# Moving a head's turned squares: sixteen transfers between partitions in place of a trip through DRAM

## The chip, the cores and the metric

The kernel runs on one core of one Trainium2 chip. The metric is the device time of one execution in microseconds. A core has five instruction queues that run beside each other and meet at semaphores: PE (matrix products, with its weight loads shown as PEld), DVE (elementwise and reductions), ACT (activation functions), POOL (GpSimd) and SP, which here only issues DMA transfers. The transfers run on sixteen DMA engines that all queues share.

## The reference, cut to what matters

Two transformer layers on 8 sequences of 512 tokens of 256 elements, in float32. Layer 0 is a rotary scan attention followed by a mixture of 16 experts with a shared expert. Layer 1 is causal attention with 16 heads of 128, followed by a feed-forward whose weights are looked up in a table of 16 values:

```python
# layer 1, attention (x: 8 x 512 x 256)
k = jnp.einsum('ihd,bpd->biph', W_K, x)
q = jnp.einsum('ihd,bpd->biph', W_Q, x)
v = jnp.einsum('ihd,bpd->biph', W_V, x)
scores = jnp.einsum('biph,biqh->biqp', k, q)
masked = scores * mask - 1e10 * (1.0 - mask)
attn = softmax(masked / sqrt(d_head), axis=-1)
z = jnp.einsum('biqp,biph->biqh', attn, v)
out = jnp.einsum('df,bqf->bqd', W_O, z_flat)
# layer 1, feed-forward
w = lut[idx]          # for gate, up and down: 688x256, 688x256, 256x688
```

The change lies in the attention of layer 1: 8 sequences x 16 heads = 128 heads.

## The kernel before, in words

Layer 0 comes first. From about 580 to 2010 us of the profiled execution the attention of layer 1 runs, in a software pipeline that is written out by hand: within it, PE, DVE, POOL and SP each keep the order of the program, and only ACT's order is left to a scheduler. The last part, some 230 us, is the feed-forward.

The outer loop goes over 64 pairs of heads (`p`), the inner one over the two heads of a pair (`e`). What a head goes through is spread over three turns of this loop; `front` is the head of the turn before, `rear` the one before that.

- `scores(i)`, for four row tiles i of 128 queries: PE makes the scores `sc` of the causal part (128 x 128(i+1)), DVE adds the mask, scales and takes the minimum of the negated row into `low`, writing `ms`; ACT exponentiates `ms` into `pr[i]` and sums the rows into `den`. `ms` has two buffers, each `pr[i]` one.
- `normalized(...)`: DVE takes reciprocals, and ACT scales the rows of `pr` into `slots`, a buffer (two of them) of 128 partitions x 4 x 10 x 32: ten squares of 128 x 128 for the causal half, cut into pieces of 32 columns.
- `squares_turned()`, for `front`, one turn later: DVE transposes each 32 x 32 block of `slots` in place (L1127). What is then still to be done is an exchange of whole blocks between groups of 32 partitions. SP writes `slots` to the DRAM tile `squares` in four transfers of 160 KB (L1130).
- `exchanged()`, later in the same turn: SP waits for those four to land and reads `squares` back into `pT` in one transfer of 640 KB (L1135). `pT` has one buffer.
- `weigh()`, for `rear`, another turn later: PE multiplies `v` with `pT` into `pz` (L1159), and ACT copies the result into `zT`.

Only the last two heads go another way, by PE transposes (`turned`), so 126 heads use the squares. Each turn also holds a share of the projections of the following pair (`pairs`, `groups`, L239), and of the output projection of the quarter of heads that was finished before (`one_out`, L1213).

SP issues the weights in the same order of the program (`load_weights`, L739 to L745; `w` for queries and keys, `wv`, `wo`), at the calls of `load_following`. `wo` has one buffer: it is loaded when the last product of a quarter (`products(3)`, within `one_out`) has been issued, and the next turn's `one_out` (`products(0)`) needs it. In such a turn the program's order is: `scores(0)` and `scores(1)`, `squares_turned`, `one_out` with the load of `wo`, ..., `scores(2)` and `scores(3)`, `exchanged`, the other loads. The framework gives the DMAs of SP eight completion semaphores in turn; a DMA that takes one again waits until the one that had it before has landed.

POOL forms the sums that the output projection takes (`zS`, L1190 to L1193), gathers rows, and once per turn takes a step of `lookups`, which builds the tables `fs` and `fd` of the feed-forward from indices: for each of 16 values a comparison (`tmp`, L956) and an addition (L959). For `fs` an operation spans 688 columns, and one value is a step; for `fd` 256 columns, and two values are a step.

Of the kernel before, what the change touches and what calls it, by code (L numbers as in the profile page):

```python
# [10 lines left out]
F32 = mybir.dt.float32  # L11
I32 = mybir.dt.int32
AF = mybir.ActivationFunctionType
# [4 lines left out]
P = 128  # L18
NB, T, D = 8, 512, 256
# [10 lines left out]
INTER = 688  # L30
# [10 lines left out]
SQ = 32  # L41
NQ = P // SQ

SLOT = {(j, i): n for n, (j, i) in enumerate((j, i) for j in range(NT) for i in range(j, NT))}
NS = len(SLOT)
# [70 lines left out]
def two_layers(ctx: ExitStack, tc: tile.TileContext, a: dict, out: bass.AP):  # L116
    nc = tc.nc
# [112 lines left out]
    class Sevens:  # L230


        def __init__(self, operands, out):
            self.operands, self.out = operands, out
# [102 lines left out]
    for b in range(1, NB):  # L337
# [8 lines left out]
            out=xs[NE * REG : NE * REG + NE * P, :].rearrange("(n p) d -> p n d", p=P),  # L346
            in_=zero.unsqueeze(1).to_broadcast([P, NE, D]),
# [377 lines left out]
    sv = tc.dram_tile([NGRP, P, 5 * 2 * DH], F32, name="sv")  # L725
    so = tc.dram_tile([NGRP, P, 5 * 2 * DH], F32, name="so")


    squares = [tc.dram_tile([P, NQ, NS * SQ], F32, name=f"squares{n}") for n in range(2)]

    wtp = ctx.enter_context(tc.tile_pool(name="wt", bufs=1))

    plain = {n: a["aqk"][n] for n in range(2)} | {"v": a["av"], "o": a["ao"]}
# [2 lines left out]
    def load_weights(n, part, first):  # L736
        f = 2 * DH if n in ("v", "o") else DH
        w = wtp.tile([P, 7, f], F32, tag=f"w{n}", name=f"w{n}", bufs=1 if n in ("v", "o") else 2)
        nc.sync.dma_start(out=w[:, :2, :], in_=plain[n][part, :, : 2 * f].rearrange("p (k f) -> p k f", k=2))  # L739
        rest = w[:, 2:, :]  # L740
        kept = made[n][part].rearrange("p (k f) -> p k f", k=5)
        if not first:
            nc.sync.dma_start(out=rest, in_=kept)
            return w, None
        nc.sync.dma_start(out=w[:, 5:, :], in_=plain[n][part, :, 2 * f :].rearrange("p (k f) -> p k f", k=2))  # L745

        return w, (lambda *eng: sums(w, *eng), lambda eng=nc.sync: eng.dma_start(out=kept, in_=rest))
# [66 lines left out]
    with tc.tile_pool(name="lk", bufs=2, side="right") as lkp, tc.tile_pool(  # L814
        name="xb", bufs=4, side="right"
# [49 lines left out]
        xb, xbT, h, hT = {}, {}, {}, {}  # L865
        weights = {}
        with tc.manual_schedule(engines={ENG.PE}):
            for s in range(NBLK + 5):
                if s % VB == 0 and s < NBLK:
                    n = min(VB, NBLK - s)  # L870
# [12 lines left out]
                if s % 12 == 2 and 0 < s // 12 <= 5:  # L883
                    n, part = ((0, 0), (1, 0), ("v", 0), (0, 1), (1, 1))[s // 12 - 1]
                    w, complete = load_weights(n, part, True)
# [40 lines left out]
    fs = w2.tile([P, 7, INTER], F32, name="fs")  # L926
# [6 lines left out]
    def lookups(pool):  # L933

        parts = [
            (fs[:, n, :], a[f"idx{w}"][c * P : (c + 1) * P, :], P)
            for n, w, c in ((W_1, 0, 0), (W_2, 0, 1), (W_4, 1, 1), (W_3, 1, 0))
        ]
        behind = []
        parts += [(fd[:k, i, :], a["idx2"][r : r + k, :], k) for i, (r, k) in enumerate(ICH)]  # L940

        def indices(dst, src, k):
            idx = pool.tile([P, INTER], I32, tag="idx", name="idx")
            nc.gpsimd.dma_start(out=idx[:k, : src.shape[1]], in_=src)
            return idx

        idx = indices(*parts[0])
        yield
        for m, (dst, src, k) in enumerate(parts):
            n = src.shape[1]  # L950
            for v in range(NLUT):
                if v == 0:
                    nc.gpsimd.tensor_scalar(dst, idx[:k, :n], 0.0, lut[:k, 0:1], ALU.is_equal, ALU.mult)
                else:
                    tmp = pool.tile([P, INTER], F32, tag="tmp", name="tmp")
                    nc.gpsimd.tensor_scalar(  # L956
                        tmp[:k, :n], idx[:k, :n], float(v), lut[:k, v : v + 1], ALU.is_equal, ALU.mult
                    )
                    nc.gpsimd.tensor_add(dst, dst, tmp[:k, :n])  # L959
                if v == NLUT - 1 and m + 1 < len(parts):  # L960
                    following = indices(*parts[m + 1])
                if n > T or v % 2:
                    if behind:
                        behind.pop(0)()
                    yield
            if dst is parts[3][0]:
                for n, c, at in ((W_1, 0, APART), (W_2, 1, APART), (W_4, 1, 0), (W_3, 0, 0)):
                    nc.gpsimd.tensor_copy(over[:, c, at : at + OVER], fs[:, n, NF * P :])
                behind = sum_steps(fs[:, :, : NF * P], nc.gpsimd)
            idx = following  # L970
# [3 lines left out]
    with tc.tile_pool(name="big", bufs=2, side="right") as big, tc.tile_pool(  # L974
        name="a1", bufs=1, side="right"
    ) as ap1, tc.tile_pool(name="lk", bufs=1, side="right") as lkp, tc.tile_pool(
        name="a2", bufs=2, side="right"
    ) as ap2, tc.tile_pool(name="pj", bufs=1, space=PSUM) as pj, tc.tile_pool(
        name="psc", bufs=2, space=PSUM
    ) as psc, tc.tile_pool(name="ptt", bufs=2, space=PSUM) as ptp, tc.tile_pool(  # L980
        name="pz", bufs=1, space=PSUM
    ) as pzp, tc.tile_pool(name="po1", bufs=1, space=PSUM) as pop:
        look = lookups(lkp)

        class Sequence:
# [87 lines left out]
                return self.v[:, j % 2, 2 * (e // 2) + j // 2, (e % 2) * DH : (e % 2 + 1) * DH]  # L1073

        class Head:
            def __init__(self, qT, kT, v, z, place, by_slots):
                self.by_slots = by_slots
                self.qT, self.kT, self.v, self.z = qT, kT, v, z
                self.pr, self.squares = {}, squares[place]
                self.low = small.tile([P, NT], F32, name="low", bufs=3)  # L1080
                self.den = small.tile([P, NT], F32, name="den", bufs=3)
                self.rd = small.tile([P, NT], F32, name="rd", bufs=3)

            def scores(self, i):

                kw = (i + 1) * P
                sc = psc.tile([P, T], F32, tag="sc", name="sc")
                nc.tensor.matmul(sc[:, :kw], self.qT[:, i * P : kw], self.kT[:, :kw], start=True, stop=True)  # L1088
                ms = ap2.tile([P, T], F32, tag="ms", name="ms")
                low = self.low[:, i : i + 1]  # L1090

                nc.vector.tensor_tensor_reduce(  # L1092
                    out=ms[:, :kw],
                    in0=sc[:, :kw],
                    in1=mask[:, T - kw :],
                    scale=-1.0 / math.sqrt(DH),
                    scalar=3e38,
                    op0=ALU.add,
                    op1=ALU.min,
                    accum_out=low,  # L1100
                )
                pr = self.pr[i] = ap2.tile([P, kw], F32, tag=f"pr{i}", name="pr", bufs=1)
                nc.scalar.activation(pr, ms[:, :kw], AF.Exp, bias=low, scale=-1.0, accum_out=self.den[:, i : i + 1])  # L1103

            def normalized(self, *tiles):

# [17 lines left out]

            def squares_turned(self):

                nc.vector.transpose(self.slots, self.slots)  # L1127
                to, slots = self.squares.rearrange("(n k) q s -> q k n s", n=NQ), self.slots.rearrange("p n s k -> p n (s k)")
                for q in range(NQ):
                    nc.sync.dma_start(out=to[q], in_=slots[q * SQ : (q + 1) * SQ])  # L1130

            def exchanged(self):

                self.pT = ap1.tile([P, NQ, NS, SQ], F32, name="pT")
                nc.sync.dma_start(out=self.pT.rearrange("p q s k -> p q (s k)"), in_=self.squares)  # L1135

            def turned(self):

                nc.vector.reciprocal(self.rd, self.den)
                self.pT = ap1.tile([P, NQ, NS, SQ], F32, name="pT")  # L1140
                for i in range(NT):
                    nc.scalar.activation(self.pr[i], self.pr[i], AF.Copy, scale=self.rd[:, i : i + 1])
                for j in range(NT):
                    pt = ptp.tile([P, T], F32, tag="pt", name="pt")
                    for i in range(j, NT):
                        nc.tensor.transpose(pt[:, i * P : (i + 1) * P], self.pr[i][:, j * P : (j + 1) * P], ident)
                    (nc.scalar.copy if j % 2 else nc.vector.tensor_copy)(
                        self.of_keys(j), pt[:, j * P :].rearrange("p (i q k) -> p i q k", q=NQ, k=SQ)
                    )
# [134 lines left out]
        for c in (1, 2, 4, 6):  # L1284
# [14 lines left out]
            out=mask[:, T - P :],  # L1299
            in_=mask[:, T - P :],  # L1300
# [6 lines left out]
        with tc.manual_schedule(engines={ENG.PE, ENG.DVE, ENG.Pool, ENG.SP}):  # L1307
# [18 lines left out]
            front = rear = None  # L1326
            for p in range(ALL):
# [4 lines left out]
                if pair % 2 == 0:  # L1332
                    z = big.tile([P, VG, T], F32, tag="big", name="zT")
                for e in range(2):
# [1 line left out]
                        *(pairs[p].of_head(n, e) for n in range(2)),  # L1336
                        lambda j, g=groups[p // 2], h=2 * (p % 2) + e: g.of_head(j, h),
                        z[:, 2 * (pair % 2) + e, :],
                        e,
                        p < ALL - 1,  # L1340
                    )
                    in_time()
# [31 lines left out]
                        one_out()  # L1374
                    head.scores(2)
                    head.scores(3)
                    if front and front.by_slots:
                        front.exchanged()
                    load_following()
                    in_time()  # L1380
                    if e and ahead:
# [12 lines left out]
                    front, rear = head, front  # L1394
# [29 lines left out]
    with tc.tile_pool(name="f1", bufs=1) as f1, tc.tile_pool(  # L1424
        name="f2", bufs=2
    ) as f2, tc.tile_pool(name="f3", bufs=3) as f3, tc.tile_pool(name="ft", bufs=1, space=PSUM) as ft, tc.tile_pool(
        name="fp", bufs=3, space=PSUM
# [65 lines left out]
        with tc.manual_schedule(engines={ENG.PE}):  # L1493
            for b in range(NB + 1):
                q = seqs[b] if b < NB else None
                front = seqs[b - 1] if b else None
# [127 lines left out]
```

## Time and profile before

| | us |
|---|---|
| median of 2 runs | 2252.16 (2249.09 to 2255.24) |
| the profiled execution | 2247.57 |
| its span, first to last instruction | 2245.8 |
| PE busy | 2108.6 (94%) |
| DVE busy | 1539.8 (69%) |
| ACT busy | 1184.2 (53%) |
| POOL busy | 868.7 (39%) |
| pT and squares of a head: first and last issue | 581.4 and 1988.0 |
| mean granted clock of PE | 0.993 of full speed |

DMA moved 363.99 MB, 162 GB/s in the mean; of HBM 241.29 MB were read and 120.72 MB written.

How to read it: busy time says how long an engine's instructions lasted, not what the time depends on. A line of waits names the engine and instruction that waited, what ended the wait, the sum in us, the number of times and the longest. `L1159` is line 1159 of the kernel before; `pT<-squares` is a transfer that writes pT and reads squares; SPq is a DMA issue on SP, whose duration is the time that it held the queue, not that of the transfer.

### The profile page before, as it was taken

The page shows a single profiled execution, that of the slowest core. Times are in us where ns is not written, and L with a number is a line of the kernel's source. Part 1 is how long each engine was busy: PE and PEld are TensorE (multiplying, and loading weights), DVE is VectorE, ACT ScalarE, POOL GpSimd, SP SyncE. Part 2 cuts the span into 40 slices and gives each one's busy share as a digit, 9 for nine tenths or more (in the row PEclk, how much of TensorE's full clock was granted, in tenths as well). Part 3 has the DMA queues.
Part 4 walks back from the last instruction along what each step waited for, and adds up shares of the span by engine and source line. Part 5 has one row for each costly group of instructions (what it writes and reads, how often), then busy time and mean ns, then how long its engine had stood idle before and what let it go on. Part 6 is the DMA issues. An engine that isn't in the chain of part 4 may idle for free.

```text
span 2245.8 us, 29655 instructions
## 1 busy us (share of the span) xinstructions
PE 2108.6 (94%) x8733; PEld 1546.5 (69%) x8733; DVE 1539.8 (69%) x3950; ACT 1184.2 (53%) x2943; POOL 868.7 (39%) x767
## 2 busy tenths in 40 slices
PE   6999998999799999999999999999999999989999
PEld 3554545886576767777777767777677777758887
DVE  6788887555567767666767766766766766758765
ACT  5767762333465556555556555556555555643211
POOL 0022233001464474565466456654535445330000
PEclk9999999999999999999999999999999999999999
DMA  6111216552567666766666666675756665520000
GB/s 194 46 69 64 75 68 238 182 162 90 168 223 229 217 208 206 221 196 218 202 213 200 221 207 207 199 227 175 216 185 208 201 219 181 177 93 11 19 19 29
DMA packets 207873, 363.99 MB, mean 162 GB/s; under 512 B 27120, under 2 KB 145264, under 8 KB 207712
## 3 DMA queue, kind: packets, MB, share of 16 engines
q1 hardware_dynamic: 197712, 333.62, 47.0%
q0 software_dynamic: 8704, 27.42, 3.6%
q8 instruction: 70, 1.15, 0.2%
q10 hardware_dynamic: 1296, 1.06, 0.1%
q14 instruction: 91, 0.75, 0.1%
HBM read 241.29 MB, written 120.72 MB: 161 GB/s over the span
## 4 chain that ended last, share of the span: by engine, by line
PE 67%; DMA 15%; DVE 12%; ACT 3%; issue 3%; SPq 1%; POOL 0%; DVEq 0%; POOLq 0%; ACTq 0%
PE pb L239 14%; PE pz L1159 11%; PE pa L239 10%; PE sc L1088 9%; DMA pT<-squares 9%; PE po L1213 6%; PE py L1482 4%; PE pgu L841 3%; DMA scale<-dscale 2%; PE pyb L859 2%; DMA squares<-slots 1%; DVE slots L1127 1%; DVE v L379 1%; PE pa L432 1%; DMA wo<-in_ao 1%
## 5 line engine op out<-in xcount | busy, mean ns | idle before, releaser
L1123 ACT ACTIVATE slots<-pr,rd 128x128 f32<-128x128 f32 x756 | 302.3, 463 | 187.1 <-DVE rd L1111 112.4
L1159 PE MATMUL pz<-pT,v 128*128 128x512 f32 (+3 forms) x1024 | 308.0, 445 | 44.9 <-DMA pT<-squares 44.8
L1088 PE MATMUL sc<-qk,qk 128*128 128x128 f32 (+3 forms) x1024 | 318.4, 433 | 0.9 <-DVE low L1092 0.8
L1159 PEld LDWEIGHTS pz<-pT,v 128*128 128x128 f32 x1024 | 194.3, 193 | 170.5 <-issue 65.6
L1103 ACT ACTIVATE pr<-ms,low 128x128 f32<-128x128 f32 (+3 forms) x512 | 282.3, 552 | 51.6 <-DVE low L1092 49.5
L1092 DVE CUSTOM_DVE_ANT_0 ms<-sc,mask 128x128 f32<-128x128 f32 (+3 forms) x512 | 238.0, 483 | 63.0 <-PE sc L1088 56.8
L956 POOL TENSOR_SCALAR tmp<-idx,lut 128x256 f32<-128x256 int32 (+2 forms) x150 | 259.5, 1730 | 12.5
L1127 DVE STREAM_TRANSPOSE slots<-slots 128x1280 f32<-128x1280 f32 x126 | 190.2, 1510 | 103.3 <-ACT slots L1123 102.3
L1166 ACT COPY zT<-pz 128x512 f32<-128x512 f32 x128 | 74.9, 585 | 288.5 <-PE pz L1159 284.5
L239 PE MATMUL pb<-tT,w 128*128 128x256 f32 x762 | 207.4, 381 | 6.3 <-DVE qk L253 5.0
L1088 PEld LDWEIGHTS sc<-qk,qk 128*128 128x128 f32 x1024 | 172.5, 191 | 47.6 <-ACT slots L1123 1.6
L632 POOL DMA_INDIRECT xs<-xn,slot x64 | 79.7, 1246 | 311.2 <-DVE share L642 121.6
L262 DVE TENSOR_TENSOR qk<-pb,u 128x512 f32<-128x512 f32 x127 | 85.3, 672 | 140.6 <-PE pb L239 140.6
L1190 POOL TENSOR_TENSOR zS<-zT 128x512 f32<-128x512 f32 x31 | 40.7, 1314 | 329.1 <-PE po L1213 329.0
L251 DVE TENSOR_TENSOR u<-pa,p 128x256 f32<-128x256 f32 x230 | 96.9, 421 | 89.7 <-ACT p L249 83.2
L239 PEld LDWEIGHTS pb<-tT,w 128*128 128x128 f32 x762 | 139.4, 191 | 25.5 <-DVE qk L253 7.5
L239 PE MATMUL pa<-xT,w 128*128 128x256 f32 x508 | 151.1, 379 | 0.0
L893 POOL DMA_INDIRECT yg<-ys,yrow x64 | 65.0, 1016 | 187.8 <-PE pu L190 138.9
L1213 PE MATMUL po<-zS,wo 128*128 128x256 f32 x512 | 125.9, 379 | 1.2 <-DVE kept L1224 1.2
L252 DVE TENSOR_TENSOR p<-pb,u 128x256 f32<-128x256 f32 x230 | 97.6, 424 | 25.2 <-DVE u L251 1.8
L1213 PE MATMUL po<-zT,wo 128*128 128x256 f32 x384 | 97.0, 390 | 17.3 <-DMA wo<-in_ao 17.3
L239 PE MATMUL pb<-wv,tT 128*128 128x256 f32 x378 | 103.8, 383 | 8.3 <-DVE qk L262 8.1
(315 smaller groups left out, 4306.3 us busy)
## 6 DMA issues: line engine op xcount, KB each, us to landing
squares<-slots SPq DMA_DIRECT2D x504, 160.0 KB
pT<-squares SPq DMA_DIRECT2D x126, 640.0 KB
w<-sqk SPq DMA_DIRECT2D x112, 320.0 KB
w<-in_aqk SPq DMA_DIRECT2D x144, 128.0 KB
wv<-sv SPq DMA_DIRECT2D x28, 640.0 KB
wo<-so SPq DMA_DIRECT2D x28, 640.0 KB
xb<-xs SPq DMA_DIRECT2D x79, 128.0 KB
ys<-yb SPq DMA_DIRECT2D x79, 128.0 KB
```

Of the source, the lines that this page charges most:

```text
L239: nc.tensor.matmul(to, lhsT, rhs, start=first, stop=True, skip_group_check=True)
L251: nc.vector.tensor_tensor(self.u2, pa[:, 1, :], p1, ALU.add)
L252: nc.vector.tensor_tensor(p1, pb[:, 0, :], self.u2, ALU.add)
L956: nc.gpsimd.tensor_scalar(tmp[:k, :n], idx[:k, :n], float(v), lut[:k, v : v + 1], ALU.is_equal, ALU.mult)
L1088: nc.tensor.matmul(sc[:, :kw], self.qT[:, i * P : kw], self.kT[:, :kw], start=True, stop=True)
L1092: nc.vector.tensor_tensor_reduce(out=ms[:, :kw], in0=sc[:, :kw], in1=mask[:, T - kw :], scale=-1.0 / math.sqrt(DH), scalar=3e38, op0=ALU.a ...
L1103: nc.scalar.activation(pr, ms[:, :kw], AF.Exp, bias=low, scale=-1.0, accum_out=self.den[:, i : i + 1])
L1123: nc.scalar.activation(to, pr, AF.Copy, scale=rd)
L1127: nc.vector.transpose(self.slots, self.slots)
L1159: nc.tensor.matmul(pz[:, :, j:, :].rearrange("p q i k -> p q (i k)"), self.v(j), self.pT[:, :, SLOT[j, j] : SLOT[j, j] + NT - j, :].rearra ...
L1213: nc.tensor.matmul(po[:, m, :], self.w[:, n, k * P : (k + 1) * P], self.sides[n][:, k, :], start=(k == 0), stop=(k == 1),)
L1482: nc.tensor.matmul(py, self.h[:, i, t * P : (t + 1) * P], fd[:, i, :], start=(i == 0), stop=(i == NI - 1))
```

## The change

The DRAM tile `squares` and the call of `exchanged` go. After the DVE transpose SP issues sixteen transfers, each from the 32 partitions of one group of `slots` to the 32 partitions of one group of `pT` (1280 bytes per partition, 40 KB in all). `pT` moves from the pool with one buffer to that with two. `ms` goes: the masked scores are written to `pr`, and the exponential works in place. The lookups of `fs` are cut into halves of 344 columns, so that `idx` and `tmp` take half the memory; two values are then a step everywhere. The lines behind these move up by 3 to 6.

```diff
-    squares = [tc.dram_tile([P, NQ, NS * SQ], F32, name=f"squares{n}") for n in range(2)]
...
         parts = [
-            (fs[:, n, :], a[f"idx{w}"][c * P : (c + 1) * P, :], P)
+            (fs[:, n, h : h + INTER // 2], a[f"idx{w}"][c * P : (c + 1) * P, h : h + INTER // 2], P)
             for n, w, c in ((W_1, 0, 0), (W_2, 0, 1), (W_4, 1, 1), (W_3, 1, 0))
+            for h in (0, INTER // 2)
         ]
...
-            idx = pool.tile([P, INTER], I32, tag="idx", name="idx")
+            idx = pool.tile([P, INTER // 2], I32, tag="idx", name="idx")
...
-                    tmp = pool.tile([P, INTER], F32, tag="tmp", name="tmp")
+                    tmp = pool.tile([P, INTER // 2], F32, tag="tmp", name="tmp")
...
-                if n > T or v % 2:
+                if v % 2:
...
-            if dst is parts[3][0]:
+            if dst is parts[7][0]:
...
-            def __init__(self, qT, kT, v, z, place, by_slots):
+            def __init__(self, qT, kT, v, z, by_slots):
...
-                self.pr, self.squares = {}, squares[place]
+                self.pr = {}
...
-                ms = ap2.tile([P, T], F32, tag="ms", name="ms")
+
+                pr = self.pr[i] = ap2.tile([P, kw], F32, tag=f"pr{i}", name="pr", bufs=1)
                 low = self.low[:, i : i + 1]
 
                 nc.vector.tensor_tensor_reduce(
-                    out=ms[:, :kw],
+                    out=pr,
...
-                pr = self.pr[i] = ap2.tile([P, kw], F32, tag=f"pr{i}", name="pr", bufs=1)
-                nc.scalar.activation(pr, ms[:, :kw], AF.Exp, bias=low, scale=-1.0, accum_out=self.den[:, i : i + 1])
+                nc.scalar.activation(pr, pr, AF.Exp, bias=low, scale=-1.0, accum_out=self.den[:, i : i + 1])
...
             def squares_turned(self):
 
+
                 nc.vector.transpose(self.slots, self.slots)
-                to, slots = self.squares.rearrange("(n k) q s -> q k n s", n=NQ), self.slots.rearrange("p n s k -> p n (s k)")
+                self.pT = ap2.tile([P, NQ, NS, SQ], F32, name="pT")
                 for q in range(NQ):
-                    nc.sync.dma_start(out=to[q], in_=slots[q * SQ : (q + 1) * SQ])
-
-            def exchanged(self):
-
-                self.pT = ap1.tile([P, NQ, NS, SQ], F32, name="pT")
-                nc.sync.dma_start(out=self.pT.rearrange("p q s k -> p q (s k)"), in_=self.squares)
+                    for n in range(NQ):
+                        nc.sync.dma_start(
+                            out=self.pT[n * SQ : (n + 1) * SQ, q], in_=self.slots[q * SQ : (q + 1) * SQ, n]
+                        )
 
             def turned(self):
 
                 nc.vector.reciprocal(self.rd, self.den)
-                self.pT = ap1.tile([P, NQ, NS, SQ], F32, name="pT")
+                self.pT = ap2.tile([P, NQ, NS, SQ], F32, name="pT")
...
-                    if front and front.by_slots:
-                        front.exchanged()
                     load_following()
```

More of the change, by code (lines that the diff above doesn't have):

```diff
@@ L1338, in two_layers @@
                         z[:, 2 * (pair % 2) + e, :],
-                        e,
                         p < ALL - 1,
```

## The prediction

> **What bounds the kernel now.** I read the page from its top. PE is busy for 94% of the span, and the chain that ended last runs over PE for two thirds and over DMA for 15%, most of it pT:
>
> ```profile
> PE 2108.6 (94%) x8733; PEld 1546.5 (69%) x8733; DVE 1539.8 (69%) x3950; ACT 1184.2 (53%) x2943; POOL 868.7 (39%) x767
> ...
> PE 67%; DMA 15%; DVE 12%; ACT 3%; issue 3%; SPq 1%; POOL 0%; DVEq 0%; POOLq 0%; ACTq 0%
> ```
>
> The chain's DMA share is no saving: when a transfer goes from the chain, the chain follows PE's work instead. What can be saved is what PE waits, so the waits of PE and of its weight loads come next:
>
> ```profile
> PEld pz L1159 <- DMA pT<-squares: 57.9, 39, 5.3
> ...
> PE pz L1159 <- DMA pT<-squares: 44.8, 34, 4.9
> ...
> PEld po L1213 <- DMA wo<-in_ao: 21.8, 20, 1.8
> ...
> PE po L1213 <- DMA wo<-in_ao: 17.3, 20, 3.4
> ```
>
> PE loses some 45 us to pT, which the change shortens, and 17 us to wo, which is loaded through the same SP queue. So the question is not only when pT lands, but what SP does first. One head in the timeline (start, duration, engine; the bracket is idle time and what ended it):
>
> ```profile
> 1210.27 1.51 DVE L1127 STREAM_TRANSPOSE slots<-slots 128x1280 f32<-128x1280 f32 x1
> ...
> 1211.84 1.87 SPq L1130 DMA_DIRECT2D squares<-slots  x4
> ...
> 1213.76 0.70 SPq L739 DMA_DIRECT2D wo<-in_ao  x1
> ...
> 1214.51 0.66 SPq L743 DMA_DIRECT2D wo<-so  x1
> ...
> 1216.27 0.32 SPq L1135 DMA_DIRECT2D pT<-squares  x1
> ...
> 1217.88 1.99 PE L1213 MATMUL po<-zT,wo 128*128 128x256 f32 x8 [0.89 <-DMA wo<-in_ao]
> ...
> 1222.29 2.42 PE L1159 MATMUL pz<-pT,v 128*128 128x512 f32 x8 [0.69 <-DMA pT<-squares]
> ```
>
> Call the first squares issue t0 (1211.84). Four squares issues take 1.88 us, 0.47 each; the last has landed at about t0+4.3, where SP goes on to pT; pT lands just before t0+10.45. wo is issued at t0+1.92, **behind the squares in SP's order**, lands just before t0+6.04, and PE stands waiting for it. I went through the timeline head by head in this way (126 heads, 11.2 us apart in the mean). In 23 of the handovers of wo from one quarter to the next it is like this one: issue near t0+1.95, PE's first product near t0+6.15, nearly always after a wait; pz follows 3.7 us after that product began. Seven others are loaded 29 us or more before their use. The pz waits split into 13.5 us in those 23 heads and 31.2 us in the other 103.
>
> **The change part by part.**
>
> *Transfers.* Out go 126 x 4 squares issues, 126 pT issues, SP's wait between them, and the second trip of 655 KB per head. In come 126 x 16 issues of 41 KB (32 partitions x 1280 B), partition to partition. DMA bytes fall by 126 x 0.655 = 83 MB of 364; that saves PE nothing by itself, as the DMA engines are busy only some 0.65 in this stage.
>
> What one of the sixteen costs SP is not in the trace. The near rows are:
>
> ```profile
> L1130 SPq DMA_DIRECT2D squares<-slots x504: 302/433/1737, 581.4 to 1982.9; - x168
> L1135 SPq DMA_DIRECT2D pT<-squares x126: 319/338/338, 588.5 to 1988.0; - x126
> ```
>
> A squares issue names 32 x 4 pieces, and back to back costs 0.47 with its gap; a pT issue, alone, costs 0.34; a 16 KB issue of eight rows (droots<-root, L532) costs 0.295. With a gap of 0.04 the bounds are 0.34 and 0.47. The new ones have a quarter of the squares' pieces, but come back to back; I take **0.38**, nearer the single ones. Sixteen: 6.1 us (5.4 to 7.5). That fits into the 11.2 us of a head beside three weight issues of about 0.45.
>
> *A wait that the change adds.* SP's DMAs take eight completion semaphores in turn, and in the changed instruction order each transfer waits for the one eight before it; behind the waiting instruction stand the rest of the head's transfers and all the weight loads. The squares row prices a landing: 2.4 us after the last of four issues. Eight issues at 0.38 take 3.0 us, so the ninth does not wait; it would if landings took over 3 us.
>
> Here a rule speaks against the change. The Trainium skill, "SBUF — State Buffer", section "The DMA setup-cost knee", says that every transfer pays about 2 us whatever its size, and "DMA: Bandwidth & Descriptors", section "Rules for kernel authors", says to coalesce, since below 64 KB one mostly pays overhead. By the rule, as an estimate, a transfer of 41 KB costs 2.0 + 0.1 us; one after the other the sixteen would take 33 us, three heads' time, which would slow the kernel by over 2000 us. But eight are in flight here, so the same price gives two rounds of 2.1 us, less than SP's 6.1 us of issuing, and the last lands at 6.1 + 2.1 = 8.2. By the row it is 6.1 + 2.4 = **8.5**. The trace already shows that 2.4 us for four transfers together, so I take the row: the overhead that counts is SP's issue, sixteen times.
>
> *What landing at t0+8.5 gains.* PE is ready for pz at t0+9.0 in the earliest twentieth of heads and at t0+10.0 in the median head (the time of pz less its wait). Summed over the 103 heads outside the handovers, a landing at 8.5 leaves 1.8 us of wait, so 31.2 - 1.8 = **29.4 us are gained** there. The weigh then waits for eight semaphores instead of one; such extra waits run ahead on PE's sequencer (51 ns each at L1213, with no gap in the matmuls behind them), so I cost them at nothing. Without that cover, four of them in 126 heads would be 26 us.
>
> *What it costs at wo.* In the 23 handovers the wo load comes after sixteen issues instead of four: at t0+6.1, not t0+1.95. It then has less before it in the DMA queues: before, 4.15 us passed from issue to use, with 640 KB of squares ahead that had landed only at t0+4.3. That leaves 1.8 us after the squares, and with its own issue and start I take 2.9 us from issue to use, between 2.3 and 4.15. So PE's first product moves from t0+6.15 to t0+9.0, a stall of 2.85 us more, and pz to t0+12.7, by when pT lies there. The pz wait of 0.59 us (13.5/23) is swallowed. Net 2.85 - 0.59 = 2.26, times 23 = **52 us lost**. PE runs in order and nothing else of it can move forward, so this is on the path.
>
> *The second pT buffer.* Transfers need not wait for the last weigh; SP waited for pz only 1.7 us at L1135 before. Nothing.
>
> *ms removed.* DVE writes its scores into pr and ACT exponentiates there. pr's old readers are ACT copies which DVE has already waited for at the transpose or the reciprocal; the changed order shows no new wait on DVE. Nothing.
>
> *Lookups in halves.* 64 + 60 more POOL operations. From the forms 128x688 and 128x256 of L956 (2600 and 1152 ns) and L959 (1646 and 728 ns), the part that doesn't scale is 294 and 184 ns: 64 x 0.294 + 60 x 0.184 = 30 us on POOL, 0.5 us per head. POOL is 39% busy and idles 329 us before zS alone; steps per head stay equal. If it had no cover, the 30 us would count. Nothing. Four index loads more on POOL's queue lie a head before use.
>
> **Sum:** -29.4 + 52 = +22.6 us. The profiled execution took 2247.57 us (span 2245.8), so 2270 on its footing; the median of the runs is 4.6 us above it, so **2275**. That is within 2% (45 us, about what a measurement of this kernel can tell from no change).
>
> **The rivals.**
>
> *SP becomes the bound at the handover* (slower). If a transfer costs what a squares issue did, 0.47, the sixteen take 7.5 us, wo is issued at 7.6 and lands at 10.5: (4.35 - 0.59) x 23 = 86 us. pT lands at 10.0, which leaves 24 us of wait in the other heads, so only 7 us are gained: +79, 2331. The same comes from landings slower than 3 us, by the eight semaphores. For it: the squares are the only burst of this kind in the stage. Against: four times as many pieces in each. It passes 2% from about 0.43 us an issue.
>
> *wo lands nearly as early* (a little faster). Issue at 0.34 and 2.3 us to land: wo at 5.4 + 2.3 = 7.7, loss (1.55 - 0.59) x 23 = 22, gain 30: -8, 2244. For it: wo no longer shares the queues with squares and pT.
>
> *All waits go* (faster by over 2%). If neither wait were left, 44.8 + 17.3 = 62 us, 2190. Against it: the wo load is plainly behind the transfers in SP's order.
>
> *The change doesn't do what it says*: DMA time hidden anyway, +-5, 2252; it needs wo's loss and pT's gain to cancel.
>
> **How the numbers follow.** The forecast with its own range 2255 to 2297 gets 0.45; SP-bound 0.30; a little faster or equal 0.20 (both small cases); all waits gone 0.05. With the end of each inside, the range is 2238 to 2345. Faster by over 2%: 0.05; within: 0.65; slower: 0.30.
>
> **What would show it.** Right: 2016 issues at L1130 of a mean near 0.34 us; PE's wait for pT down from 45 to under 10 us and its wait for wo up from 17 to about 80 us, in 23 places of 3 to 4 us; HBM bytes written down by 83 MB. Wrong: a wait for wo that stays under 30 us (the queue order was cheap), waits of SP for its own transfers of over 2 us a head (the eight semaphores decide), or waits of pz for pT that remain.

## The result and the profile after

The changed kernel took 2557.41 us (2551.29 to 2563.54), the kernel before 2252.16: a ratio of 1.137, with a 95% interval of 1.1343 to 1.1396. It is 305 us slower, where 23 us were forecast.

The page of the changed kernel: busy time, what HBM moved, and the chain by engine.

```profile
PE 2217.2 (87%) x8733; PEld 1610.1 (63%) x8733; DVE 1541.5 (60%) x3950; ACT 1184.6 (46%) x2943; POOL 894.1 (35%) x895
...
HBM read 158.71 MB, written 38.14 MB: 77 GB/s over the span
...
PE 47%; SPq 20%; DMA 16%; DVE 10%; issue 4%; ACT 3%; POOL 0%; another core or an unknown queue 0%; DVEq 0%; POOLq 0%; ACTq 0%
```

The change did what it says: writes to HBM fell by 82.6 MB, reads by as much. The profiled execution is 316 us longer than that of before (spans 2561.8 and 2245.8 us): PE stands idle 207 us longer in it, and its busy time is 109 us longer for the same 8733 products. Both parts need an explanation.

SP's issuing, which held 1% of the chain before, now holds 20%. One row says why. Its three numbers are the shortest, median and longest issue in ns:

```profile
L1130 SPq DMA_DIRECT2D pT<-slots x2016: 507/589/1850, 581.6 to 2306.0; - x184
```

The issues now span 1724 us where they spanned 1401, with the same number of heads: 13.8 us a head instead of 11.2. The waits of PE, of its weight loads and of SP in the changed kernel:

```profile
PEld pz L1156 <- issue: 237.0, 367, 7.6
...
PE pz L1156 <- DMA pT<-slots: 187.6, 62, 7.2
...
PE po L1210 <- DMA wo<-in_ao: 86.3, 23, 9.7
...
SPq L1130 <- DVE slots L1126: 168.1, 58, 8.5
...
SPq L1130 <- DMA wv<-sv: 44.3, 27, 3.1
```

PE waits for pT four times as long as before (45 us), and five times as long for wo (17 us), in exactly 23 places. The first line is mostly also a wait for pT, under another name: the weight loads of pz wait for eight semaphores, most of them in instructions of their own (482 at this line, where there were 2), and what passes there is booked as "issue" (65.6 us before). Weight loads run beside products, so the PEld and PE lines cover in part the same time and must not be added. SP in turn waited for the transpose for 538 us in 113 heads before, and for 168 us in 58 heads now: in many heads the transposed squares are ready and SP is not. Among SP's waits there is none for its own transfers to pT. One head's time on SP, from the timeline:

```profile
1308.15 0.53 SPq L736 DMA_DIRECT2D w<-in_aqk  x1
1308.72 0.43 SPq L740 DMA_DIRECT2D w<-sqk  x1
...
1311.16 10.01 SPq L1130 DMA_DIRECT2D pT<-slots  x16
...
1321.27 0.53 SPq L736 DMA_DIRECT2D w<-in_aqk  x1
1321.84 0.43 SPq L740 DMA_DIRECT2D w<-sqk  x1
...
1322.52 7.71 SPq L1130 DMA_DIRECT2D pT<-slots  x12
1322.84 2.39 PE L1156 MATMUL pz<-pT,v 128*128 128x512 f32 x8 [1.02 <-DMA pT<-slots]
```

Sixteen issues take 10.0 us and the weight loads follow. Ahead of the first of these heads SP still waits 2.0 us for the transpose; ahead of the second it goes on within 0.25 us of its last load.

### The profile page after: what moved, and what is told of

The parts are those of the page before. It is cut to its first block, busy times and chain, and to the rows that moved or that the text cites. A ratio compares the mean times of both kernels' runs of the same rounds, so it can differ in the third digit from the quotient of the medians.

```text
span 2561.8 us, 31889 instructions
## 1 busy us (share of the span) xinstructions
PE 2217.2 (87%) x8733; PEld 1610.1 (63%) x8733; DVE 1541.5 (60%) x3950; ACT 1184.6 (46%) x2943; POOL 894.1 (35%) x895
## 4 chain that ended last, share of the span: by engine, by line
PE 47%; SPq 20%; DMA 16%; DVE 10%; issue 4%; ACT 3%; POOL 0%; another core or an unknown queue 0%; DVEq 0%; POOLq 0%; ACTq 0%
SPq L1130 18%; PE pb L239 8%; PE pa L239 7%; DMA wv<-sv 7%; PE pz L1156 7%; PE po L1210 6%; PE sc L1086 5%; PE py L1476 3%; DMA wo<-in_ao 3%; PE pgu L838 3%; DMA pT<-slots 2%; DMA scale<-dscale 2%; PE pyb L856 1%; DVE slots L1126 1%; ACT slots L1121 1%
## 5 line engine op out<-in xcount | busy, mean ns | idle before, releaser
L1156 PE MATMUL pz<-pT,v 128*128 128x512 f32 (+3 forms) x1024 | 366.6, 509 | 195.4 <-DMA pT<-slots 187.6
L1156 PEld LDWEIGHTS pz<-pT,v 128*128 128x128 f32 x1024 | 219.9, 222 | 357.8 <-issue 237.0
L1101 ACT ACTIVATE pr<-pr,low 128x128 f32<-128x128 f32 (+3 forms) x512 | 282.5, 553 | 53.7 <-DVE low L1091 51.8
L954 POOL TENSOR_SCALAR tmp<-idx,lut 128x344 f32<-128x344 int32 (+2 forms) x210 | 276.9, 1319 | 18.0
L1091 DVE CUSTOM_DVE_ANT_0 pr<-sc,mask 128x128 f32<-128x128 f32 (+3 forms) x512 | 238.8, 483 | 62.9 <-PE sc L1086 59.7
L1210 PE MATMUL po<-zT,wo 128*128 128x256 f32 x384 | 123.2, 470 | 86.3 <-DMA wo<-in_ao 86.3
L1210 PEld LDWEIGHTS po<-zT,wo 128*128 128x128 f32 x384 | 87.8, 235 | 110.6 <-DMA wo<-in_ao 85.4
L1188 POOL TENSOR_TENSOR zS<-zT,zS 128x512 f32<-128x512 f32 x31 | 39.3, 1267 | 303.2 <-ACT zT L1163 303.2
```

Source lines behind the costliest of these rows:

```text
L954: nc.gpsimd.tensor_scalar(tmp[:k, :n], idx[:k, :n], float(v), lut[:k, v : v + 1], ALU.is_equal, ALU.mult)
L1091: nc.vector.tensor_tensor_reduce(out=pr, in0=sc[:, :kw], in1=mask[:, T - kw :], scale=-1.0 / math.sqrt(DH), scalar=3e38, op0=ALU.add, op1= ...
L1101: nc.scalar.activation(pr, pr, AF.Exp, bias=low, scale=-1.0, accum_out=self.den[:, i : i + 1])
L1156: nc.tensor.matmul(pz[:, :, j:, :].rearrange("p q i k -> p q (i k)"), self.v(j), self.pT[:, :, SLOT[j, j] : SLOT[j, j] + NT - j, :].rearra ...
L1210: nc.tensor.matmul(po[:, m, :], self.w[:, n, k * P : (k + 1) * P], self.sides[n][:, k, :], start=(k == 0), stop=(k == 1),)
```

## The experiments

Four theories for the loss. **Theory 1**: an issue between partitions is dear in itself. **Theory 2**: the DMA engines move 41 KB between so few partitions slowly, and the issue waits for them. **Theory 3**: the eight semaphores hold back transfers. **Theory 4**: another part of the change costs the time.

### The disputed cost by itself

A program of bursts only (three of each form; the next burst waits for the one before):

```python
                for k in range(n):
                    transfer(eng, dst, k)
                if where == "sbuf":
                    nc.vector.tensor_copy(small, dst[:, :, :16])
...
        def across(eng, d, k):
            q, n = k // 4, (k + 1) % 4
            eng.dma_start(out=d[n * Q : (n + 1) * Q, q], in_=src[q * Q : (q + 1) * Q, n])
```

> A program of its own that does nothing but issue DMAs in bursts on an otherwise idle core; of the reference it computes nothing and writes zeros. Each form is issued three times in a burst of eight (four for the forms that span 128 partitions, sixteen for the writes to DRAM): 32 partitions to 32 other partitions, 1280 bytes each, as in the changed kernel; the same with 256 bytes; within one group of partitions; 16, 64 and 128 partitions to as many; 32 partitions to DRAM in one piece each and in four pieces each; DRAM to 32 and to 128 partitions; DRAM to DRAM; and the first form from the queues of ACT and POOL. Theory 1 (the issue of a transfer between partitions is dear in itself): 0.55 to 0.63 us per issue for the first form and for 256 bytes alike, and 0.45 or less for one piece to DRAM. Theory 2 (the DMA engines' pace at 41 KB between few partitions): 256 bytes cost 0.4 us or less per issue, and 32 partitions to DRAM as much as to partitions. Theory 3 (eight semaphores): on the idle core the first eight issues are at 0.35 us each.

The rows of the forms, each: shortest, median, longest issue in ns. `across` is the changed kernel's form, `fifth` the same with 256 bytes, `sixtyfour` and `allrows` span 64 and 128 partitions; then 32 partitions to DRAM in one and in four pieces, DRAM to 32 partitions, DRAM to DRAM; last, `across` from ACT and from POOL.

```profile
L42 SPq DMA_DIRECT2D across<-src x24: 507/590/629, 8.1 to 31.0; - x24
...
L46 SPq DMA_DIRECT2D fifth<-src x24: 507/590/592, 35.9 to 58.4; - x24
...
L57 SPq DMA_DIRECT2D sixtyfour<-src x24: 461/596/597, 118.5 to 141.8; - x24
...
L61 SPq DMA_DIRECT2D allrows<-src x12: 465/599/603, 146.9 to 162.7; - x12
...
L65 SPq DMA_DIRECT2D todram<-src x48: 302/419/485, 166.6 to 195.8; - x48
...
L70 SPq DMA_DIRECT2D todramfour<-src x12: 303/430/496, 200.0 to 213.6; - x12
...
L74 SPq DMA_DIRECT2D fromdram<-drin x24: 303/420/429, 221.3 to 243.9; - x24
...
L82 SPq DMA_DIRECT2D dramdram<-drin x24: 469/591/592, 277.4 to 305.3; - x24
...
L42 ACTq DMA_DIRECT2D onact<-src x24: 514/612/613, 310.9 to 334.2; - x24
...
L42 POOL DMA_DIRECT2D onpool<-src x24: 498/498/631, 339.5 to 359.8; - x24
```

In these bursts bytes, rows and pieces hardly matter to what an issue costs. The two ends do: **0.42 us where one end is DRAM and the other SBUF, 0.59 us where both are SBUF or both are DRAM**, with some 0.04 us between two issues. A burst of eight on an idle core costs that already (in most bursts only its first issue is cheaper, 0.51 us). Theories 2 and 3 fall.

The two prices are not the whole of it: behind much that is still under way an issue was dearer. In the bursts of four writes with four pieces the fourth takes 0.47 to 0.50 us; in the prediction's timeline of the kernel before, the two loads of wo behind the four squares take 0.70 and 0.66 us, though they go from DRAM to SBUF; and in the changed kernel's timeline above, the load right behind sixteen transfers takes 0.53. The profile's list of issues gives 1.9 us from issue to landing for `across`.

### The transfers undone, the rest kept

```diff
...
+                for q in range(NQ):
+                    nc.sync.dma_start(out=to[q], in_=slots[q * SQ : (q + 1) * SQ])
+
+            def exchanged(self):
+
                 self.pT = ap2.tile([P, NQ, NS, SQ], F32, name="pT")
-                for q in range(NQ):
-                    for n in range(NQ):
-                        nc.sync.dma_start(
-                            out=self.pT[n * SQ : (n + 1) * SQ, q], in_=self.slots[q * SQ : (q + 1) * SQ, n]
-                        )
+                nc.sync.dma_start(out=self.pT.rearrange("p q s k -> p q (s k)"), in_=self.squares)
...
+                    if front and front.by_slots:
+                        front.exchanged()
```

> The changed kernel with the transfers alone undone: four writes to DRAM and one read back, at their old places; the second pT buffer, the exponential in place and the halved lookups stay. Theories 1 to 3 all put the loss on the sixteen transfers: the time is that of the kernel before or up to 10 us less, 2240 to 2255. Theory 4 (the loss comes from the other edits): it stays above 2400.

Measured 2255.87 us, 1 us above the range named, and a ratio to before of 1.0011 (0.9999 to 1.0024). Theory 4 falls: together the second buffer, the exponential in place and the halved lookups cost some 5 us at most, by that interval. PE's waits for pT and wo are about as before (44.8 and 17.3 us):

```profile
PE pz L1160 <- DMA pT<-squares: 45.2, 34, 4.5
PE po L1214 <- DMA wo<-in_ao: 20.1, 19, 3.3
```

### A fifth of the bytes

```diff
-  out=self.pT[n * SQ : (n + 1) * SQ, q], in_=self.slots[q * SQ : (q + 1) * SQ, n]
+  out=self.pT[n * SQ : (n + 1) * SQ, q, :2], in_=self.slots[q * SQ : (q + 1) * SQ, n, :2]
```

> The changed kernel with sixteen transfers of 256 instead of 1280 bytes per partition (two of the ten squares; the rest of pT is zeros or old data, and pT lies in two fixed buffers). Theory 1, the count of issues decides: 2520 to 2560, as with full transfers. Theory 2, the bytes decide: 2230 to 2300. Theory 3, landings decide: in between, since each transfer lands earlier.

Measured 2551.55 us, 1.131 (1.1263 to 1.1357): four fifths of the transfers' bytes gone, and the time is within 6 us of the changed kernel's. Its issue row shows the same 589 ns:

```profile
L1132 SPq DMA_DIRECT2D pT<-slots x2016: 507/589/1818, 583.5 to 2295.8; - x184
```

### Eight and twelve of the sixteen

```diff
-                    for n in range(NQ):
+                    for n in range(q % 2, NQ, 2):     # eight
+                    for n in range(NQ - 1):           # twelve, in the other run
```

> The changed kernel with eight of the sixteen transfers, each of full size (half of pT is zeros, in two fixed buffers). Theory 1: SP issues 5.1 us per head and 1.7 us of loads, well below a head's 11 us, so SP is no bound and PE is again: 2220 to 2260. Theory 3: about the same, since eight need no semaphore twice. Theory 4: above 2400.

> The changed kernel with twelve of the sixteen transfers (a quarter of pT is zeros, in two fixed buffers). SP issues 7.6 us a head and 1.6 us of loads, below 11.2, so by theory A it is not yet the bound: wo is issued at t0+7.6, used at t0+10.8, which is 4.7 us of PE in 23 heads, less 0.6 of pT, so +94; pT lands at t0+9.5, leaving 10 of 31 us: +73, 2325. If the time grew evenly with the transfers from eight (2280) to sixteen (2557), it would be 2418.

Eight took 2280.6 us, 1.0112 (1.009 to 1.0134); twelve took 2399.43, 1.0668 (1.0632 to 1.0703). PE's waits from 600 to 2000 us with eight, where none for pT is left among the first lines, and to 2250 us with twelve:

```profile
PE po L1211 <- DMA wo<-in_ao: 72.6, 23, 6.0
```

```profile
PE po L1211 <- DMA wo<-in_ao: 121.7, 23, 8.9
PE pz L1157 <- DMA pT<-slots: 38.3, 21, 4.9
```

Eight is the prediction's mechanism in pure form: the wait for pT is gone, -45 us, and the load of wo, behind 5.1 us of issues, is used at t0+8.0 to 8.8 in most of the 23 handovers and costs +55. The sum of the two, +11, is what PE's idle time grew by in the profiled execution (148 us, where it was 137). That execution, the fastest of six, is 20 us longer than the profiled one of before; the other 9 us are longer busy time of PE. The median of the runs is 26 us above before, and 20 beyond the range's end of 2260. With twelve wo is issued at t0+7.6 and used near t0+11, as expected, and its wait is 104 us above that of before; but 2325 was expected and 2399 measured, nearer to even growth. pT's wait did not fall as the table of heads had it: SP stood 38 us behind wv's loads and 17 behind wo's, and began late in some heads. But most of what the forecast lacks is again busy time: PE's idle time grew by 95 us, its busy time by 59 (2167.9 us, where it was 2108.6), and the forecast had no term for the second.

### The load of wo ahead of the transfers

```diff
                         front.squares_turned()      # the transpose alone
                     one_out()
+                    if front and front.by_slots:
+                        front.sent()                # the sixteen transfers
```

> The changed kernel with one move: SP issues the load of wo ahead of a head's sixteen transfers (the transfers are called after one_out; DVE's order stays). Theory A (SP's sixteen issues of 0.634 us, 10.1 us, with its weight loads fill a head's time, and PE waits for pT): only the wait changes its name; wo's 86 us go, pT's grow, and the time stays at 2500 to 2557. Theory B (the loss is mainly wo behind the transfers): 86 us go, 2470 or less.

Measured 2466.88 us, 1.0968 (1.0931 to 1.1005). Theory B had the number: 90 us go with wo's place. But the other 218 stay, and there theory A holds. PE's wait for wo is no longer listed; the one for pT is (PE from 600 to 2250 us, then SP over the whole run):

```profile
PE pz L1159 <- DMA pT<-slots: 197.1, 82, 6.7
```

```profile
SPq L1133 <- DVE slots L1126: 47.8, 32, 2.6
SPq L1133 <- DMA wv<-sv: 40.0, 28, 2.4
SPq L1133 <- DMA wo<-so: 24.3, 25, 2.1
```

SP now waits for the transpose for only 48 us in 126 heads. A head takes 12.9 us; sixteen issues of 0.634 us are 10.1, some three weight loads of 0.48 are 1.4, and the waits above are 0.9. That makes 12.4 of 12.9, of which only 0.4 is a wait for another engine: SP sets the pace.

### Eight from SP, eight from POOL

```diff
-                        nc.sync.dma_start(
+                        (nc.gpsimd if n % 2 else nc.sync).dma_start(
```

> The sixteen direct transfers, eight issued by SP and eight by POOL, with the load of wo first. SP then needs 5.1 us a head and POOL 3.9 us (0.49 each in the bursts); pT lands near t0+7, before PE asks for it at t0+9 to 10. Both waits of PE go: 45 to 60 us less than the kernel before, 2190 to 2210. If POOL comes late to its share (it stands in its own order, busy for half of the time, and waits for the transpose), pT lands late and POOL's sums for the output projection as well: above 2260.

Measured 2347.64 us, 1.0444 (1.0417 to 1.047). It is better than sixteen on SP, and still slower than before: from 600 to 2250 us PE waits for pT twice as long as before.

```profile
PE pz L1159 <- DMA pT<-slots: 83.2, 30, 6.8
```

POOL's timeline shows the case that was named as the other outcome:

```profile
1304.10 1.43 POOL L954 TENSOR_SCALAR tmp<-idx,lut 128x344 f32<-128x344 int32 x1
1305.62 0.92 POOL L957 TENSOR_TENSOR fs<-fs,tmp 128x344 f32<-128x344 f32 x1
1306.64 1.44 POOL L954 TENSOR_SCALAR tmp<-idx,lut 128x344 f32<-128x344 int32 x1
1308.16 0.92 POOL L957 TENSOR_TENSOR fs<-fs,tmp 128x344 f32<-128x344 f32 x1
1309.04 0.54 POOL L1133 DMA_DIRECT2D pT<-slots  x1
1312.41 3.44 POOL L1133 DMA_DIRECT2D pT<-slots  x7 [2.83 <-issue]
```

SP began this head's transfers at 1307.18; POOL was in a lookup until 1309.1, and after its first transfer it stood still for 2.8 us, which the profile puts down to no one; its last came 8 us after SP's first. What that gap is stays open, and so does whether ACT's queue would serve better than POOL's.

### Four blocks copied by ACT

The four blocks that stay in their group of partitions need no transfer:

```diff
-                        nc.sync.dma_start(
+                        (nc.scalar.copy if n == q else nc.sync.dma_start)(
```

> Direct transfers with wo's load first, but the four blocks that stay in their own group of partitions are copied by ACT (some 0.45 us each); SP keeps twelve. SP: 12 x 0.634 = 7.6 us and 1.6 us of loads, under a head's 11 us; pT lands near t0+9.5, about when PE asks for it, and wo isn't waited for: 2215 to 2245, which would show that twelve issues cost nothing once wo is ahead of them. If SP's load, not wo's place, made the run with twelve slow, it stays above 2330.

Measured 2261.99 us, 1.0058 (1.0037 to 1.008). All sixteen blocks arrive, wo comes first, SP issues twelve: the 150 us of the run with twelve are nearly gone, so most of that loss came with wo's place. It is 17 us above its range. PE (600 to 2250 us) now also waits for DVE in the projections, 24 us in two lines where the kernel before shows 2.5, and ACT's copies add 230 us of work; that the one comes from the other is likely but was not tested.

```profile
PE pz L1159 <- DMA pT<-slots: 41.1, 22, 4.6
PE pb L239 <- DVE v L253: 13.7, 11, 2.1
PE pb L239 <- DVE qk L253: 10.5, 18, 1.1
```

### A faster version: through DRAM, in a better order

What was learned serves the way through DRAM, whose eight or five issues cost SP less. First only wo's load ahead of the four writes, then also the read in four parts, then the four reads directly behind the writes:

```diff
+                        front.sent()                # e5: the four writes, behind one_out()
...
+                for q in range(NQ):                 # e8: four reads in place of one
+                    nc.sync.dma_start(out=pT[:, q], in_=self.squares[:, q])
...
+                        front.exchanged()           # e10: the reads right after sent()
```

> The way through DRAM (second pT buffer, in-place exponential and halved lookups kept) with the load of wo ahead of the four squares writes. wo's wait of 20 us goes, and pT, with no wo load before it in the queues, lands some 1 us earlier in 23 heads: 15 to 30 us less than the kernel before, 2222 to 2240. If another wait takes their place (pT in the same heads), 2245 to 2255.

Measured 2221.22 us, 0.9874 (0.9853 to 0.9896), 1 us below the range named.

> The way through DRAM with wo's load first, and the read of pT in four parts, each issued when its own write has landed (in the bursts a write of 160 KB landed 2.6 us after its issue). The four reads are then issued between t0+2.6 and t0+4.5 and should land near t0+7, three us earlier than the one read; PE asks for pT at t0+9 to 10. So pT's wait goes, 30 to 40 us less than with the one read (2221): 2180 to 2195. If pieces of 1280 instead of 5120 bytes take the DMA engines so much longer that nothing lands earlier: 2215 to 2230.

Measured 2214.59 us, 0.9838 (0.9819 to 0.9858): a gain of only 7 us, just beyond the noise or not at all, since the two intervals touch. That is the edge of the second guess's range, but not for its reason. What is left of pT's wait sits in few heads, as the weight loads of PE show one by one: waits of 3.5 to 4.9 us in the first head, in one near the end, and in seven between them some 177 us apart, one for each change of sequence. In the turns of these seven SP loads wo and other weights between the four writes and the four reads.

> The run with the read in four parts, and these four issued by SP directly behind the four writes, ahead of any weight load that the turn adds later. In that run eight waits of PE for pT of 3.5 to 4.9 us were left, one per sequence, in turns in which wo is loaded between the writes and the reads; they go, some 30 us: 2180 to 2190. If the waits come from the weight traffic itself and not from the place of the reads: 2205 to 2220.

Measured 2192.74 us, 0.9745 (0.9726 to 0.9763), 3 us above the range named: 57 us less than the kernel before and 365 less than the changed one. PE's waits for pT before these two steps (e5) and after them (e10), from 600 to 2250 us:

```profile
PE pz L1163 <- DMA pT<-squares: 32.0, 16, 3.8
```

```profile
PE pz L1165 <- DMA pT<-squares: 16.5, 9, 2.9
```

One wait at each change of sequence remains, of 1.8 to 2.9 us on the weight loads, so the place of the reads was part of it. In these turns the reads go out 6.2 to 7.6 us after the first write, where 2.2 us is the median of the others: they wait for the writes to land, and SP has issued loads of wo or wv some 2 us ahead of those writes. So the weight traffic is the likely rest; no run tests it.

## Why the prediction was wrong

The step that failed is the price of one transfer's issue. It was bounded by 0.34 and 0.47 us and taken at 0.38; it is 0.63 (0.59 and a gap of 0.04). Both bounds came from rows in which one end of the transfer is DRAM, and the count of pieces was taken for what sets the price. In the bursts it hardly does (0.42 us for one piece, 0.43 for four), and what the change did alter, both ends in SBUF in place of one, does. The trace of before had no issue with both ends alike, so the upper bound should have been open there. The prediction's own timeline, with 0.70 and 0.66 us for the loads of wo, had two rows above that bound.

A second term is missing from its sum, without a reason given: PE's products were taken to last as long as before. They took 109 us longer, a third of the 316 (the last section shows where).

Point by point:

- **The range** was cut at the squares row. The rival "SP becomes the bound at the handover" had the mechanism, at a price a quarter too low, and so 2331.
- **wo behind the transfers** was right, in place and kind: 23 handovers. Taking it away brings 90 us (e4). The forecast of 2.9 us from wo's issue to its use was near: 2.9 in the changed kernel, about 3.2 in the run with eight. That its sign, "about 80 us", met the 86.3 measured is luck: it was worked out with wo used at t0+9.0, and wo is used at t0+13.0 and later, as 16 issues of 0.634 and those 2.9 us give. PE merely reaches that product later too.
- **pT landing at t0+8.5** was wrong, by the issue's price. In the bursts landing is 1.9 us after the issue, less than the 2.4 taken. With 0.634 us the prediction's own sum gives 10.1 + 1.9 = 12.0 for pT, where its table of heads leaves 156 us of wait in place of 31, and wo used at t0+13.0: 125 + (6.85 - 0.59) x 23 = 269 us, 2521. That this comes within 36 us of the result does not show that the sum is complete. It is a sum of waits, and PE's idle time grew by 207 us, not by 269; the rest is the longer busy time. A fixed table of heads also leaves out that each late head moves the next one. How these share in the difference stays open.
- **"That fits into the 11.2 us of a head"** was wrong for the same reason: 10.1 + 1.4 us is above 11.2, and e4 shows SP setting the pace.
- **The eight semaphores** do not hold the transfers against each other, as said: SP shows no wait for pT's own transfers. But a transfer does wait for a weight load that is still under way (44 us at wv). Its data does not depend on that load, so it most likely takes the semaphore that the load has; the prediction missed this.
- **The rule against small transfers** was set aside for the row, by the right argument on landings: about 2 us each by the Trainium skill ("SBUF — State Buffer", section "The DMA setup-cost knee"), 1.9 measured, and with several in flight they are hidden. But the advice to coalesce (the Trainium skill, "DMA: Bandwidth & Descriptors", section "Rules for kernel authors") was right here, for the issue's price and not for the landing's.
- **The other edits at nothing** was right: 1.0011.
- **One small misreading**: the seven other loads of wo are used 25 to 28 us after they were issued, not 29 or more. Nothing rests on it.

## What to carry to other kernels

Before a few DMAs are replaced by many, price the issue on the queue that sends them, from a row with the same kinds of memory at both ends, and set the sum per loop against the loop's time: here that sum was the bound, not bytes or landing. When no such row exists, leave the bound open upward. And look at what is queued behind: moving one load ahead of the four writes made the kernel 28 us faster here, and ahead of the sixteen transfers 90 us. Where the change can make the main engine wait in stretches of some us, do not take its busy time as fixed.

## What the runs showed of the hardware that was not expected

In bursts on an idle core an issue on SP costs 0.59 us with both ends in SBUF or both in DRAM, and 0.42 with one end in each, for 8 KB as for 160 KB. For the transfers between partitions the price is 0.61 us on ACT's queue and 0.50 on POOL's.

PE also gets slower where it waits. The stage before and in the changed kernel (stretch, length, busy time of PE, PEld, DVE, ACT, POOL with counts, granted clock, DMA share, GB/s):

```profile
581.00:1988.00 1407.00, 1332.06 (x5573) 1005.97 (x5574) 953.57 (x2568) 797.96 (x2255) 762.46 (x661) 0.99 0.66 206
```

```profile
581.00:2311.00 1730.00, 1443.32 (x5599) 1070.48 (x5599) 957.26 (x2574) 803.54 (x2266) 795.75 (x794) 0.92 0.40 120
```

The stretch is 323 us longer; 111 of these are PE busy for longer with the same products, at a clock of 0.92 in place of 0.99. The longer products are those behind the waits. The first two products of a head's pz, where PE waits for pT, took 622 ns in the mean and take 729; those of the scores of the same form, with no wait ahead of them, stay at 592 (before, then changed):

```profile
L1159 PE MATMUL pz<-pT,v 128*128 128x512 f32 x256 | 138.2, 622 | 44.9 <-DMA pT<-squares 44.8
L1088 PE MATMUL sc<-qk,qk 128*128 128x512 f32 x256 | 130.7, 592 | 0.0
```

```profile
L1156 PE MATMUL pz<-pT,v 128*128 128x512 f32 x256 | 164.5, 729 | 195.4 <-DMA pT<-slots 187.6 <-DMA w<-in_aqk 4.8 <-issue 3.0
L1086 PE MATMUL sc<-qk,qk 128*128 128x512 f32 x256 | 130.7, 592 | 0.0
```

One wait close up, of 3.2 us before the product at 1281.0: the clock is full during the wait, half for some us just behind it, then full again.

```profile
1278.00:1281.00 3.00, 0.00 (x0) 0.03 (x1) 1.98 (x4) 0.41 (x3) 2.81 (x3) 1.00 0.25 61
1282.10:1285.50 3.40, 3.40 (x9) 2.48 (x9) 0.00 (x0) 0.58 (x1) 3.13 (x4) 0.50 0.92 282
1286.00:1290.00 4.00, 4.00 (x20) 2.98 (x19) 2.94 (x8) 2.70 (x7) 2.62 (x3) 1.00 0.82 295
```

In this stage of the changed kernel the granted clock falls to a half 52 times, for 3.4 or 6.8 us, once for 10.2. Each time PE had been idle for over 2 of the 6.8 us before; over the whole stage the median of such windows is 0.3 us of idle time. Over the whole execution PE runs at half clock for 35 us before, 67 with eight transfers, 207 with twelve, 214 with wo ahead, and 292 in the changed kernel, where its idle time is 137, 148, 232, 277 and 345 us. How much of the 305 us the lower clock adds, and how much of it falls into time that PE would have waited anyway, no run separates.
